# The end of attention in an adaLN block: operand placement, banks, order and softmax scaling of the last batch's outputs

## The chip, the cores and the metric

The kernel runs on one core of one Trainium2 chip. A core has five engines with instruction queues of their own: TensorE (PE: matmuls; its weight loads, PEld, overlap them), VectorE (DVE), ScalarE (ACT), GpSimd (POOL) and SyncE (SP, which here issues most DMAs). They run beside each other and wait for one another through semaphores. The metric is the device time of one execution in microseconds.

## The reference

All in float32. B = 8 batches of S = 1024 tokens, width D = 256, 16 heads of 64, 8 experts.

```python
mod = (silu(c) @ wmod).reshape(8, 6, 1, 256)      # sa, ca, ga, sb, cb, gb per batch
h = layernorm(x) * (1 + ca) + sa
q, k, v = heads(h @ w_qkv)                         # 16 heads of 64
o = softmax(q @ k.T / 8) @ v
x = x + ga * (concat(o) @ w_o)
h = layernorm(x) * (1 + cb) + sb                   # 8192 tokens
scores = softmax(h @ router_w + router_b)          # 8192 x 8
G, idx = top_k(scores.T, 512)                      # 512 tokens for each expert
y = scatter_add over idx of G * (relu(h[idx] @ w1 + b1) @ w2 + b2)
out = x + gb * y
```

The choice of 512 of 8192 tokens for each expert needs the scores of all eight batches: no expert can start before the last token's score.

## The kernel before

**Attention.** Work is cut into 128 units (`NSU`): a unit is one batch b, one pair of heads p (8 pairs, `NP`) and one half h of the 1024 queries. Inside a unit eight chunks of 128 keys pass through scores (PE, L372), a copy to SBUF (ACT, L381), a running maximum (DVE, L386), subtraction of the row maximum (DVE, L434), exp (ACT, L437), the product with the values (PE, L446) and the sum of the exponentials (POOL, L465). The loop counts g, four steps to a unit. The order of the instructions on each engine is the order in which the program writes them down; side work is hung into it by hand with `at(g, slot, function, ...)`, where the slots of one step are load, m1, post, pool and m2, in this order.

**Softmax denominators.** A unit's sums are added over the partitions by PE (`den_out`, L481), copied (L489) and stored to DRAM (`den_store`, L498). For each pair they come back spread over 128 partitions (`den_load`, L505), DVE inverts them and they are stored again (`den_inv`, L512), and come back once more broadcast to all rows (`den_spread`, L521, the tile `rb`). POOL multiplies the pair's output `oT` by them (`den_mul`, L527), and `oT` goes to DRAM (`oT_d`, L531). For the last pair of the last batch the same trip is made for each half by itself: `last_load_den` (L538), `last_inv` (L544 to L551, the tile `rb_last`) and `last_mul` (DVE, L557). Half 0 goes over SP's queue, half 1 over ACT's. Pairs 6 and 7 of the last batch stay on the chip (`at_hand`).

**Outputs of a batch.** For batches 0 to 6, attention of batch b + 1 carries them along, a tile of 128 tokens at a time: `out_load` reads x and the eight pairs (`ot`), `out_proj` multiplies by `wo` (PE, L582), then come the gate, the residual and the statistics, `out_norm` (rstd and three passes on POOL), `out_turn` (two tiles transposed, ACT copies), `out_route` (router logits, PE L637, and DVE L642 to L644), `out_exp` (ACT, L652), `out_score` (DVE: sum L659, reciprocal L660, and L663, which writes exp times reciprocal into the last 8 columns of the token's `row`), and `out_store` (POOL copies these columns into the table `scores`, L670; SP stores the row, L671).

**The last batch** has no attention after it. At the loop's end `last_gates` scales `wo` by the batch's gate (DVE, L690), `last_load` (L697) reads pairs 0 to 5 of each token tile, 384 KB for each of eight tiles, at steps 4*NSU+3 and 4*NSU+4, and L827 reads x in two halves. Then PE adds up the tiles: pairs 0 to 6 of tiles 0 to 3, then pair 7 of these, which needs `last_mul(0)`, then tiles 4 to 7 with all pairs (`add_pairs`, L854). The eight sums lie in `pos`, in banks of four pools of PSUM. `add_x` (DVE L862, statistics L116 and L117, rstd on POOL, L106 and L108), `norm` (L871 on DVE, L875 and L876 on POOL for even tiles and on DVE for odd ones), `turn`, `route` and `score` follow in an order written out by hand (L897 to L904).

**After it.** Four transposes (L983) turn the table into `p_sc`, DVE takes the upper halves of the score bits (`half`, L995), and a search finds the 512th largest score of each expert; then the tokens are gathered and the FFN of the eight experts runs. `rows_d` holds the tokens' rows in DRAM for this.

Of the kernel before, what the change touches and what calls it, by code (L numbers as in the profile page):

```python
# [28 lines left out]
F32 = mybir.dt.float32  # L29
# [10 lines left out]
P = 128  # L40
# [4 lines left out]
def adaln_block(  # L45
# [90 lines left out]
    H0 = 4  # L136
    wqs = [wp.tile([P, KC, 3, n, N], F32, name=f"wq{i}") for i, n in enumerate((H0, H - H0))]
    wo = wp.tile([P, NP, D], F32, name="wo")
# [300 lines left out]
    def values_mm(u, c):  # L439
        b, p, h = unit(u)  # L440
        if c == 0:
            avs[u] = ps_av.tile([P, QB], F32, tag="av", name=f"av{u}")
        v, pT = vs[b, p // 2], probs[u, c]
        for j in range(2):
            hh = 2 * (p % 2) + j
            nc.tensor.matmul(  # L446
                avs[u][j * N : (j + 1) * N, :], v[:, c, hh * N : (hh + 1) * N], pT[:, j, :],
                start=(c == 0), stop=(c == NT - 1),
            )

    def values_out(u):
        b, p, h = unit(u)
        if h == 0:
            oTs[b, p] = work.tile([P, S], F32, tag="oT", name=f"oT{b}_{p}", bufs=2)
        nc.scalar.copy(oTs[b, p][:, h * QB : (h + 1) * QB], avs.pop(u))  # L455
# [11 lines left out]
    den_d, rden_d = {}, {}  # L467
    at_hand = {(B - 1, p): None for p in (NP - 2, NP - 1)}

# [16 lines left out]
    def den_store(u, pd):  # L486
# [6 lines left out]
        else:  # L493
            if h == 0:
                den_d[b, p] = dram.tile([2, S], F32, name=f"den_d{b}_{p}")
            dst = den_d[b, p][:, h * QB : (h + 1) * QB]
        eng = nc.scalar if u == NSU - 1 else nc.sync
        eng.dma_start(dst.rearrange("j (i q) -> j i q", i=2), den[::32, :])  # L498
# [55 lines left out]

    def last_mul(h):
        half = oTs[B - 1, NP - 1][:, h * QB : (h + 1) * QB]
        nc.vector.tensor_mul(half, half, last_d[h])  # L557
# [97 lines left out]
    def out_score(b, t):  # L655
        n = f"{b}_{t}"
        ex = o_x.pop((b, t))
        den = small.tile([P, 2], F32, tag="rden2", name=f"rd{n}")
        nc.vector.tensor_reduce(den, ex, AX.X, ALU.add)  # L659
        nc.vector.reciprocal(den, den)  # L660
        for i in range(2):
            row = o_h[b, t + i]
            nc.vector.tensor_scalar_mul(row[:, D:], ex[:, i, :], den[:, i : i + 1])  # L663

    def out_store(b, t):
        tt = b * NT + t
        for i in range(2):
            row = o_h.pop((b, t + i))
            ct, ci = divmod(tt + i, KT)
            nc.gpsimd.tensor_copy(scores[:, ci, :, ct], row[:, D:])  # L670
            nc.sync.dma_start(rows_d[(tt + i) * P : (tt + i + 1) * P, :ROW], row)  # L671
# [21 lines left out]

    def last_load(t):
        b = B - 1
        o_t[b, t] = work.tile([P, NP - 2, P], F32, tag="p", name=f"ot{b}_{t}", bufs=PB)
        nc.sync.dma_start(  # L697
            o_t[b, t], oT_d[b][: NP - 2, :, t * P : (t + 1) * P].rearrange("n p s -> p n s")
        )

# [60 lines left out]
    at(4 * NSU - 2, "load", last_mods)  # L761
    for t in range(NT):
        at(4 * NSU + (3 if t < NT // 2 else 4), "load", last_load, t)
    at(4 * NSU + 4, "load", last_load_den, 0)
# [3 lines left out]
    with tc.manual_schedule():  # L768
# [14 lines left out]
        while g < 4 * NSU + LAG or steps:  # L783
# [12 lines left out]
            if gm == 3 and late:  # L796
                subtract(*late[1])
            run(g, "m1")
            run(g, "post")
# [4 lines left out]

            alone = turn and g not in taken
            if 0 <= u1 < NSU:
                for c in (2 * gm1, 2 * gm1 + 1):
                    if alone and c % 2:
                        max_turn(u)
                    values_mm(u1, c)  # L810
# [13 lines left out]
        b = B - 1  # L824
        for i in range(2):
            xs = work.tile([P, 4, D], F32, tag="p", name=f"xs{i}", bufs=PB)
            nc.sync.dma_start(  # L827
                xs, x[b, i * 4 * P : (i + 1) * 4 * P, :].rearrange("(t p) d -> p t d", p=P)
            )
            for t in range(4):  # L830
                o_x[b, 4 * i + t] = xs[:, t : t + 1, :]
        pd_last = ps_m.tile([P, QH], F32, tag="mm", name="pd_last")
# [6 lines left out]

        pos = []  # L840
        for pool, tag, n in (
            (ps_s, "s", 2), (ps_s, "s", 2), (ps_b, "less", 2), (ps_m, "mm", 1), (ps_av, "av", 1)
        ):
            po = pool.tile([P, n, 512], F32, tag=tag, name=f"po_last{len(pos)}")
            pos += [po[:, i, :D] for i in range(n)]

        def add_pairs(t, p0, p1):
            for p in range(p0, p1):
                src = (
                    o_t[b, t][:, p, :] if p < NP - 2  # L850
                    else (at_hand[b, p] if p == NP - 2 else oTs[b, p])[:, t * P : (t + 1) * P]
                )
                for m in range(2):
# [5 lines left out]
        def add_x(t):  # L859

            x1 = o_x[b, t]
            nc.vector.tensor_add(x1[:, 0, :], x1[:, 0, :], pos[t])  # L862
            nc.sync.dma_start(out[b, t * P : (t + 1) * P, :], x1[:, 0, :])
            mv = stats_of(small, x1, 1, f"b{b}_{t}")
            o_h[b, t] = mv, rstd_of(small, mv, 1, f"b{b}_{t}")

        def norm(t):
            mv, rs = o_h[b, t]
            row = small.tile([P, ROW], F32, tag="row", name=f"row{b}_{t}", bufs=6)
            h2 = row[:, :D]  # L870
            nc.vector.tensor_scalar(  # L871
                h2, o_x.pop((b, t))[:, 0, :], mv[:, 0, 0:1], rs, op0=ALU.subtract, op1=ALU.mult
            )
            eng = nc.vector if t % 2 else nc.gpsimd
            eng.tensor_tensor(h2, h2, mods[b][:, 2, :], ALU.mult)  # L875
            eng.tensor_tensor(h2, h2, mods[b][:, 1, :], ALU.add)  # L876
            o_h[b, t] = row

        def turn(t):
            out_turn(ps_s, b, t, tag="s")  # L880

        def route(t):
            out_route(ps_s, b, t, tag="s")

# [4 lines left out]

        half = NT // 2  # L890
        for t in range(half):
            add_pairs(t, 0, NP - 1)
        last_mul(0)
        for t in range(half):
            add_pairs(t, NP - 1, NP)
        last_mul(1)
        for f, *args in (  # L897
            (add_x, 0), (add_x, 1), (norm, 0), (add_pairs, 4, 0, NP), (add_x, 2), (norm, 1),
            (add_x, 3), (norm, 2), (add_pairs, 5, 0, NP), (turn, 0), (norm, 3), (add_x, 4),
            (route, 0), (norm, 4), (add_pairs, 6, 0, NP), (turn, 2), (add_x, 5), (norm, 5),  # L900
            (score, 0), (route, 2), (add_pairs, 7, 0, NP), (turn, 4), (add_x, 6), (norm, 6),
            (score, 2), (add_x, 7), (route, 4), (norm, 7), (score, 4), (turn, 6), (route, 6),
            (score, 6),
        ):  # L904
            f(*args)
# [33 lines left out]
    with tc.tile_pool(name="search", bufs=2) as se, tc.tile_pool(  # L939
# [49 lines left out]
        with tc.manual_schedule():  # L989
# [4 lines left out]
            low = po_.tile([P, K], U16, name="low")  # L994
            nc.vector.tensor_single_scalar(half[:, 0, :], bits, LB, op=ALU.logical_shift_right)  # L995
            nc.vector.tensor_copy(top, half[:, 0, :])
# [268 lines left out]
```

## Time and profile before

| | us |
|---|---|
| median of 3 runs (lowest, highest) | 3542.25 (3541.15, 3543.44) |
| the profiled execution, and its span | 3543.85, 3542.1 |
| busy in the span: PE, DVE, POOL, ACT | 3446.4, 2847.9, 2655.7, 2437.0 |
| loop of attention ends on PE, tile 7's last matmul ends, `half` ends | about 3182, 3221, 3233.6 |

The span is what the profiler recorded from the first to the last instruction; the profiled execution took 1.75 us more. The page's second part cuts the span into 40 slices of 88.6 us; a digit is the busy share of a slice in tenths, and PEclk the clock that TensorE was granted:

```profile
PE   8999999999999999999999999999999999995898
DVE  6888888888888888888888888888888888886332
PEclk9999999999999999999999999999999999996899
```

Slices 1 to 35 are attention, slice 36 holds the last batch's outputs and the beginning of the search, and the rest is the search, the gathering and the FFN. A line of the timeline gives the start, the length, the engine (SPq and ACTq: a DMA issued from that queue), the line of the code, the operation with its tiles, the number of instructions joined in it, and in brackets the idle time of the engine before it and what ended that.

### The profile page before, as it was taken

How to read it: one execution, taken by the hardware profiler on the slowest of the kernel's cores; microseconds unless marked ns; L12 is line 12 of the kernel's file. 1: busy time of each engine (PE TensorE's matmuls, PEld its weight loads, DVE VectorE, ACT ScalarE, POOL GpSimd, SP SyncE). 2: the span in 40 equal slices, each digit the busy share in tenths (PEclk: the TensorE clock that was granted, in tenths of full speed). 3: DMA queues.
4: the chain of work that ended last, by engine and by line, in shares of the span. 5: the costliest groups of instructions: out<-in, count | busy, mean ns of one | idle time of the engine just before them, and what ended most of it. 6: DMA issues, size and time to landing. Idle time of an engine off the chain costs nothing. (4 is left out here: it accounts for less than half of the span.)

```text
span 3542.1 us, 54875 instructions
## 1 busy us (share of the span) xinstructions
PE 3446.4 (97%) x20991; PEld 1456.2 (41%) x20991; DVE 2847.9 (80%) x3566; ACT 2437.0 (69%) x2998; POOL 2655.7 (75%) x1535
## 2 busy tenths in 40 slices
PE   8999999999999999999999999999999999995898
PEld 3333333334433343334433343334433343434566
DVE  6888888888888888888888888888888888886332
ACT  5877877777777777777777777777777777760111
POOL 3788777978788887978788888978788888881233
PEclk9999999999999999999999999999999999996899
DMA  4010012011210112011210112011210112124342
GB/s 79 14 42 31 25 46 65 26 44 44 64 54 27 52 50 65 30 41 44 64 52 28 51 50 65 31 40 47 62 51 31 48 52 58 40 78 161 95 104 43
DMA packets 190139, 185.44 MB, mean 52 GB/s; under 512 B 49308, under 2 KB 167596, under 8 KB 189748
## 3 DMA queue, kind: packets, MB, share of 16 engines
q1 hardware_dynamic: 173916, 160.54, 16.5%
q0 software_dynamic: 7168, 12.72, 1.8%
q10 hardware_dynamic: 8792, 8.67, 0.8%
q8 instruction: 165, 2.70, 0.3%
q14 instruction: 98, 0.80, 0.1%
HBM read 127.06 MB, written 63.21 MB: 54 GB/s over the span
## 5 line engine op out<-in xcount | busy, mean ns | idle before, releaser
L465 POOL TENSOR_TENSOR acc<-acc,p 128x1024 f32<-128x1024 f32 x764 | 1811.6, 2371 | 351.0 <-ACT p L437 317.6
L381 ACT COPY p<-s 128x1024 f32<-128x1024 f32 x1024 | 994.4, 1018 | 402.6 <-PE s L372 395.3
L434 DVE TENSOR_TENSOR p<-p,less 128x1024 f32<-128x1024 f32 x1024 | 1205.9, 1209 | 28.3 <-PE less L431 25.7
L386 DVE TENSOR_TENSOR top<-top,s 128x1024 f32<-128x1024 f32 x768 | 936.4, 1219 | 268.8 <-ACT p L381 228.8
L437 ACT ACTIVATE p<-p 128x1024 f32<-128x1024 f32 x1024 | 1041.8, 1057 | 72.8 <-DVE p L434 72.6
L372 PE MATMUL s<-qk,qk 64*128 64x512 f32 x4096 | 1020.3, 611 | 15.3 <-DVE parts L412 12.2
L446 PE MATMUL av<-p,v 128*64 128x512 f32 x4096 | 969.1, 593 | 1.8 <-ACT oT L455 1.8
L372 PEld LDWEIGHTS s<-qk,qk 64*128 64x128 f32 x4096 | 359.2, 186 | 512.7 <-issue 220.9
L337 PE MATMUL pq<-hT,wq 128*64 128x512 f32 x2048 | 497.0, 606 | 2.2 <-ACT hT L302 2.2
L446 PEld LDWEIGHTS av<-p,v 128*64 128x64 f32 x4096 | 279.7, 137 | 456.4 <-issue 355.4
L462 POOL TENSOR_TENSOR acc<-p,p 128x1024 f32<-128x1024 f32 x128 | 304.0, 2375 | 162.7 <-ACT p L437 162.7
L337 PEld LDWEIGHTS pq<-hT,wq 128*64 128x64 f32 x2048 | 124.9, 136 | 340.7 <-issue 204.6
L354 PE MATMUL pv<-wq,hT 128*64 128x256 f32 x2048 | 249.2, 385 | 0.0
L582 PE MATMUL po<-wo,ot 128*64 128x256 f32 x1792 | 205.7, 382 | 0.0
L354 PEld LDWEIGHTS pv<-wq,hT 128*64 128x64 f32 x2048 | 135.7, 136 | 152.3 <-issue 61.2
L1185 ACT ACTIVATE h<-ph,b_sb 128x512 f32<-128x512 f32 (+1 forms) x72 | 46.0, 640 | 209.2 <-PE ph L1181 209.2
L404 DVE TENSOR_REDUCE tt<-tt 128x8 f32<-128x1024 f32 x112 | 137.7, 1229 | 56.9 <-PE tt L393 56.8
L386 DVE TENSOR_TENSOR top<-p,s 128x1024 f32<-128x1024 f32 x128 | 155.5, 1215 | 11.9 <-ACT p L381 11.9
L393 PEld LDWEIGHTS tt<-ident,top 128*128 128x128 f32 x1024 | 109.6, 140 | 109.8 <-DVE top L386 109.8
L527 POOL TENSOR_TENSOR oT<-oT,rb 128x1024 f32<-128x1024 f32 x63 | 150.2, 2384 | 0.8 <-issue 0.8
L582 PEld LDWEIGHTS po<-wo,ot 128*64 128x64 f32 x1792 | 123.5, 137 | 66.2 <-issue 9.4
L393 PE MATMUL tt<-ident,top 128*128 128x128 f32 x1024 | 139.9, 280 | 4.7 <-DVE top L386 4.6
(191 smaller groups left out, 2298.1 us busy)
## 6 DMA issues: line engine op xcount, KB each, us to landing
rb<-rden_d SPq DMA_DIRECT2D x126, 256.0 KB
oT_d<-oT SPq DMA_DIRECT2D x62, 512.0 KB
ot<-oT_d SPq DMA_DIRECT2D x56, 512.0 KB
rows_d<-row SPq DMA_DIRECT2D x64, 132.0 KB
rows_d<-gb_d SPq DMA_DIRECT2D x8, 1024.0 KB
w<-in_L_ffn_w_dram ACTq DMA_DIRECT2D x8, 1024.0 KB
w<-in_L_ffn_w_dram SPq DMA_DIRECT2D x8, 1024.0 KB
lnx<-in_L_attn_inputs_dram SPq DMA_DIRECT2D x28, 256.0 KB
```

What stands on the lines that cost most here:

```text
L337: nc.tensor.matmul(pq[m * N : (m + 1) * N, :], wq_of(k, a, 2 * p + m), hTs[b][:, k, sl], start=(k == 0), stop=(k == KC - 1),)
L354: nc.tensor.matmul(pv[m * N : (m + 1) * N, i, :], hTs[b][:, k, t0 : t0 + N], wq_of(k, 2, 4 * g, 4), start=(k == 0), stop=(k == KC - 1),)
L372: nc.tensor.matmul(ps[:, j, :], kt[r, c * P : (c + 1) * P], qt[r, h * QB : (h + 1) * QB], start=True, stop=True,)
L381: nc.scalar.copy(probs[u, c], ps)
L386: nc.vector.tensor_tensor(tops[u], probs[u, 0] if c == 1 else tops[u], ps, ALU.max)
L393: nc.tensor.transpose(turned[u][:, 4 * j + t, :], top[:, j, t * P : (t + 1) * P], ident)
L434: nc.vector.tensor_tensor(probs[u, c], probs[u, c], less[u], ALU.add)
L437: nc.scalar.activation(probs[u, c], probs[u, c], AF.Exp)
L446: nc.tensor.matmul(avs[u][j * N : (j + 1) * N, :], v[:, c, hh * N : (hh + 1) * N], pT[:, j, :], start=(c == 0), stop=(c == NT - 1),)
L462: nc.gpsimd.tensor_tensor(sums[u], pts[0], pts[1], ALU.add)
L465: nc.gpsimd.tensor_tensor(sums[u], sums[u], pt, ALU.add)
L582: nc.tensor.matmul(po[m * N : (m + 1) * N, :], ot[:, p, m * N : (m + 1) * N], wo[:, p, :], start=(p == 0), stop=(p == NP - 1),)
```

## The change

- **Scaling of the scores.** `out_score` no longer writes into the rows. A new function `to_table` multiplies both tiles' exponentials by their reciprocals in one instruction, straight into `scores`: on POOL (in `out_store`) for batches 0 to 6, on DVE (in `out_score`) for the last. POOL then copies from the table into the rows, not the other way.
- **Operands of the last batch.** Pairs 4 to 7 stay on the chip: 4 and 5 in one tile of the tag `hT`, which is free by then, so their stores to `oT_d` go. Pairs 0 to 3 come in one load of 2 MB into the place of `wq1`, and x in one load of 1 MB into a buffer of the tag `v`, both on SP at step 4*NSU-6, where eight loads of 384 KB and two of x stood at and behind 4*NSU+3.
- **Queue.** The denominators of unit 126 are stored from ACT's queue, as those of unit 127 were.
- **Banks.** The last unit's values are summed in a bank of `ps_s`. The eight tiles lie as the list in the diff says, the transposes in `ps_m` and the logits in `ps_av`. Rows of tiles 6 and 7 lie in the place of `wq0`.
- **Order.** Pairs 0 to 6 are done for three tiles ahead of pair 7, not four. `last_mul(1)` stands behind `norm(1)`. `turn(4)` stands ahead of tile 7's matmuls. The hand-written list is rewritten to match.
- **Normalization.** Two instructions of DVE for a tile, (x - mean) * (1 + cb) in `add_x` and then * rstd + sb in `norm`, take the place of three on DVE or POOL.
- **`half`** is written in two parts of 256 columns.
- In the main loop, the transposes of the maxima go between the value products only where projections stand in the same step (`between`).

```diff
     H0 = 4
-    wqs = [wp.tile([P, KC, 3, n, N], F32, name=f"wq{i}") for i, n in enumerate((H0, H - H0))]
+    wqs = [
+        wp.tile([P, KC, 3, n, N], F32, tag=f"wq{i}", name=f"wq{i}")
+        for i, n in enumerate((H0, H - H0))
+    ]
     wo = wp.tile([P, NP, D], F32, name="wo")
 ...
     def values_mm(u, c):
         b, p, h = unit(u)
         if c == 0:
-            avs[u] = ps_av.tile([P, QB], F32, tag="av", name=f"av{u}")
+            pool, tag = (ps_s, "s") if u == NSU - 1 else (ps_av, "av")
+            avs[u] = pool.tile([P, QB], F32, tag=tag, name=f"av{u}")
 ...
     def values_out(u):
         b, p, h = unit(u)
-        if h == 0:
+        if h == 0 and (b, p) == (B - 1, NP - 4):
+            two = work.tile([P, 2, S], F32, tag="hT", name=f"oT{b}_{p}")
+            oTs[b, p], oTs[b, p + 1] = two[:, 0, :], two[:, 1, :]
+        elif h == 0 and (b, p) != (B - 1, NP - 3):
             oTs[b, p] = work.tile([P, S], F32, tag="oT", name=f"oT{b}_{p}", bufs=2)
         nc.scalar.copy(oTs[b, p][:, h * QB : (h + 1) * QB], avs.pop(u))
 ...
     den_d, rden_d = {}, {}
-    at_hand = {(B - 1, p): None for p in (NP - 2, NP - 1)}
+    at_hand = {(B - 1, p): None for p in range(NP - 4, NP)}
 ...
-        eng = nc.scalar if u == NSU - 1 else nc.sync
+        eng = nc.scalar if u >= NSU - 2 else nc.sync
         eng.dma_start(dst.rearrange("j (i q) -> j i q", i=2), den[::32, :])
 ...
     def last_mul(h):
+        at_hand[B - 1, NP - 1] = oTs[B - 1, NP - 1]
         half = oTs[B - 1, NP - 1][:, h * QB : (h + 1) * QB]
         nc.vector.tensor_mul(half, half, last_d[h])
     def out_score(b, t):
         n = f"{b}_{t}"
-        ex = o_x.pop((b, t))
+        ex = o_x[b, t]
         den = small.tile([P, 2], F32, tag="rden2", name=f"rd{n}")
         nc.vector.tensor_reduce(den, ex, AX.X, ALU.add)
         nc.vector.reciprocal(den, den)
-        for i in range(2):
-            row = o_h[b, t + i]
-            nc.vector.tensor_scalar_mul(row[:, D:], ex[:, i, :], den[:, i : i + 1])
+        o_x[b, t] = ex, den
+        if b == B - 1:
+            to_table(b, t, nc.vector)
+    def to_table(b, t, eng):
+        ex, den = o_x.pop((b, t))
+        ct, ci = divmod(b * NT + t, KT)
+        eng.tensor_tensor(
+            scores[:, ci : ci + 2, :, ct], ex, den.unsqueeze(2).to_broadcast([P, 2, E]), ALU.mult
+        )
     def out_store(b, t):
+        if b < B - 1:
+            to_table(b, t, nc.gpsimd)
         tt = b * NT + t
         for i in range(2):
             row = o_h.pop((b, t + i))
             ct, ci = divmod(tt + i, KT)
-            nc.gpsimd.tensor_copy(scores[:, ci, :, ct], row[:, D:])
+            nc.gpsimd.tensor_copy(row[:, D:], scores[:, ci, :, ct])
             nc.sync.dma_start(rows_d[(tt + i) * P : (tt + i + 1) * P, :ROW], row)
 ...
-    def last_load(t):
-        b = B - 1
-        o_t[b, t] = work.tile([P, NP - 2, P], F32, tag="p", name=f"ot{b}_{t}", bufs=PB)
-        nc.sync.dma_start(
-            o_t[b, t], oT_d[b][: NP - 2, :, t * P : (t + 1) * P].rearrange("n p s -> p n s")
-        )
+    last = {}
+    def last_load():
+        b, n = B - 1, NP - 4
+        last["oT"] = wp.tile([P, n, S], F32, tag="wq1", name="oT_last")
+        nc.sync.dma_start(last["oT"], oT_d[b][:n].rearrange("n p s -> p n s"))
+        last["x"] = work.tile([P, NT, D], F32, tag="v", name="x_last")
+        nc.sync.dma_start(last["x"], x[b].rearrange("(t p) d -> p t d", p=P))
 ...
-    for t in range(NT):
-        at(4 * NSU + (3 if t < NT // 2 else 4), "load", last_load, t)
+    at(4 * NSU - 6, "load", last_load)
     at(4 * NSU + 4, "load", last_load_den, 0)
 ...
         b = B - 1
-        for i in range(2):
-            xs = work.tile([P, 4, D], F32, tag="p", name=f"xs{i}", bufs=PB)
-            nc.sync.dma_start(
-                xs, x[b, i * 4 * P : (i + 1) * 4 * P, :].rearrange("(t p) d -> p t d", p=P)
-            )
-            for t in range(4):
-                o_x[b, 4 * i + t] = xs[:, t : t + 1, :]
+        rows_last = wp.tile([P, 2, ROW], F32, tag="wq0", name="rows_last")
         pd_last = ps_m.tile([P, QH], F32, tag="mm", name="pd_last")
 ...
-        pos = []
-        for pool, tag, n in (
-            (ps_s, "s", 2), (ps_s, "s", 2), (ps_b, "less", 2), (ps_m, "mm", 1), (ps_av, "av", 1)
+        pos = {}
+        for pool, tag, ts in (
+            (ps_s, "s", (0, 1)), (ps_m, "mm", (2,)), (ps_av, "av", (3,)), (ps_s, "s", (4, 6)),
+            (ps_b, "less", (5, 7)),
         ):
-            po = pool.tile([P, n, 512], F32, tag=tag, name=f"po_last{len(pos)}")
-            pos += [po[:, i, :D] for i in range(n)]
+            po = pool.tile([P, len(ts), 512], F32, tag=tag, name=f"po_last{ts[0]}")
+            for i, t in enumerate(ts):
+                pos[t] = po[:, i, :D]
         def add_pairs(t, p0, p1):
             for p in range(p0, p1):
-                src = (
-                    o_t[b, t][:, p, :] if p < NP - 2
-                    else (at_hand[b, p] if p == NP - 2 else oTs[b, p])[:, t * P : (t + 1) * P]
-                )
+                src = last["oT"][:, p, :] if p < NP - 4 else at_hand[b, p]
+                src = src[:, t * P : (t + 1) * P]
 ...
         def add_x(t):
-            x1 = o_x[b, t]
+            x1 = last["x"][:, t : t + 1, :]
             nc.vector.tensor_add(x1[:, 0, :], x1[:, 0, :], pos[t])
             nc.sync.dma_start(out[b, t * P : (t + 1) * P, :], x1[:, 0, :])
             mv = stats_of(small, x1, 1, f"b{b}_{t}")
-            o_h[b, t] = mv, rstd_of(small, mv, 1, f"b{b}_{t}")
+            rs = rstd_of(small, mv, 1, f"b{b}_{t}")
+            if t < NT - 2:
+                row = small.tile([P, ROW], F32, tag="row", name=f"row{b}_{t}", bufs=6)
+            else:
+                row = rows_last[:, t - NT + 2, :]
+            nc.vector.scalar_tensor_tensor(
+                row[:, :D], x1[:, 0, :], mv[:, 0, 0:1], mods[b][:, 2, :],
+                op0=ALU.subtract, op1=ALU.mult,
+            )
+            o_h[b, t] = row, rs
         def norm(t):
-            mv, rs = o_h[b, t]
-            row = small.tile([P, ROW], F32, tag="row", name=f"row{b}_{t}", bufs=6)
-            h2 = row[:, :D]
-            nc.vector.tensor_scalar(
-                h2, o_x.pop((b, t))[:, 0, :], mv[:, 0, 0:1], rs, op0=ALU.subtract, op1=ALU.mult
-            )
-            eng = nc.vector if t % 2 else nc.gpsimd
-            eng.tensor_tensor(h2, h2, mods[b][:, 2, :], ALU.mult)
-            eng.tensor_tensor(h2, h2, mods[b][:, 1, :], ALU.add)
+            row, rs = o_h[b, t]
+            nc.vector.scalar_tensor_tensor(
+                row[:, :D], row[:, :D], rs, mods[b][:, 1, :], op0=ALU.mult, op1=ALU.add
+            )
             o_h[b, t] = row
         def turn(t):
-            out_turn(ps_s, b, t, tag="s")
+            out_turn(ps_m, b, t, tag="mm")
         def route(t):
-            out_route(ps_s, b, t, tag="s")
+            out_route(ps_av, b, t, tag="av")
 ...
-        half = NT // 2
-        for t in range(half):
+        n = 3
+        for t in range(n):
             add_pairs(t, 0, NP - 1)
         last_mul(0)
-        for t in range(half):
+        for t in range(n):
             add_pairs(t, NP - 1, NP)
-        last_mul(1)
         for f, *args in (
-            (add_x, 0), (add_x, 1), (norm, 0), (add_pairs, 4, 0, NP), (add_x, 2), (norm, 1),
-            (add_x, 3), (norm, 2), (add_pairs, 5, 0, NP), (turn, 0), (norm, 3), (add_x, 4),
-            (route, 0), (norm, 4), (add_pairs, 6, 0, NP), (turn, 2), (add_x, 5), (norm, 5),
-            (score, 0), (route, 2), (add_pairs, 7, 0, NP), (turn, 4), (add_x, 6), (norm, 6),
-            (score, 2), (add_x, 7), (route, 4), (norm, 7), (score, 4), (turn, 6), (route, 6),
-            (score, 6),
+            (add_x, 0), (add_pairs, 3, 0, NP), (add_x, 1), (norm, 0), (add_x, 2), (norm, 1),
+            (last_mul, 1), (norm, 2), (add_x, 3), (add_pairs, 4, 0, NP), (norm, 3), (turn, 0),
+            (add_x, 4), (norm, 4), (add_pairs, 5, 0, NP), (add_x, 5), (route, 0), (norm, 5),
+            (turn, 2), (add_pairs, 6, 0, NP), (score, 0), (add_x, 6), (route, 2), (norm, 6),
+            (turn, 4), (add_pairs, 7, 0, NP), (score, 2), (add_x, 7), (route, 4), (norm, 7),
+            (score, 4), (turn, 6), (route, 6), (score, 6),
         ):
             f(*args)
 ...
-            nc.vector.tensor_single_scalar(half[:, 0, :], bits, LB, op=ALU.logical_shift_right)
+            for s in (slice(0, K // 2), slice(K // 2, K)):
+                nc.vector.tensor_single_scalar(
+                    half[:, 0, s], bits[:, s], LB, op=ALU.logical_shift_right
+                )
 ...
```

## The prediction

> **What bounds the kernel now.** I read the page's first rows, then a table of busy time by stretches, then the timeline of the last 60 us of attention. The stretches first (columns: window, length, busy time of each engine with its instruction count, granted TensorE clock, DMA share, GB/s):
>
> ```profile
> 3000.00:3100.00 100.00, 99.55 (x606) 40.03 (x604) 83.90 (x98) 75.62 (x93) 81.73 (x45) 1.00 0.13 41
> 3150.00:3200.00 50.00, 40.52 (x310) 18.09 (x311) 34.69 (x39) 25.07 (x32) 33.34 (x16) 1.00 0.46 116
> 3200.00:3220.00 20.00, 18.59 (x178) 11.92 (x175) 14.02 (x41) 1.56 (x4) 9.51 (x20) 0.91 0.25 82
> 3220.00:3240.00 20.00, 8.63 (x128) 6.04 (x124) 12.09 (x50) 2.54 (x8) 7.63 (x32) 0.61 0.69 239
> ```
>
> Inside attention TensorE (PE, the first engine column) is busy 99.6 of 100 us, so what the change does on DVE and GpSimd (POOL) there is worth something only if PE waited for it. From 3150 on PE has gaps. The timeline tells what they wait for (start, length, engine, line, idle before and its releaser):
>
> ```profile
> 3177.78 2.48 DVE L663 TENSOR_SCALAR row<-ex,rd 128x8 f32<-128x8 f32 x2
> 3180.18 4.51 DVE L690 TENSOR_TENSOR wo<-wo,mod 128x1024 f32<-128x1024 f32 x2
> ...
> 3182.24 4.07 SPq L697 DMA_DIRECT2D ot<-oT_d  x4
> 3182.53 0.60 ACTq L498 DMA_DIRECT2D den_d<-den  x1
> ...
> 3187.45 0.38 ACTq L538 DMA_DIRECT2D dq_last<-den_d  x1
> ...
> 3192.50 0.43 DVE L544 RECIPROCAL dq_last<-dq_last 128x8 f32<-128x8 f32 x2 [7.81 <-DMA dq_last<-den_d]
> ...
> 3198.84 1.29 DVE L557 TENSOR_TENSOR oT<-oT,rb_last 128x512 f32<-128x512 f32 x2 [5.91 <-DMA rows_d<-row]
> 3199.59 2.73 PE L854 MATMUL po_last<-wo,oT 128*64 128x256 f32 x16 [4.26 <-DVE oT L557]
> ```
>
> The denominators of pair 7 make two trips through DRAM, and their 2 to 4 KB stand behind 3.1 MB of `ot` loads: 4.9 us from store to the next issue (3182.53 to 3187.45), 4.7 more to the reciprocal. PE does pairs 0–6 of four tiles meanwhile, runs dry, waits 4.26 us, and restarts slowly. After the last tile:
>
> ```profile
> 3223.35 0.41 DVE L862 TENSOR_TENSOR xs<-xs,po_last 128x256 f32<-128x256 f32 x1
> ...
> 3226.78 0.69 PE L618 MATMUL pth<-ident,row 128*128 128x128 f32 x2 [3.06 <-DVE row L876]
> ...
> 3228.21 1.03 PE L637 MATMUL pl<-rw,h2T 128*64 128x8 f32 x16
> ...
> 3231.93 0.33 POOL L670 COPY scores<-row 128x8 f32<-128x8 f32 x2
> ...
> 3232.91 0.69 DVE L995 TENSOR_SCALAR half<-p_sc 128x512 int32<-128x512 int32 x1 [1.65 <-PE p_sc L983]
> ```
>
> Tile 7's matmuls end at 3220.99 (tile timeline), and its add waits until 3223.35 behind tile 2/3's scores on DVE. A serial chain then runs to the table of score bits (`half`, done 3233.60). From there on the same search and FFN run in both kernels, so I place the end of `half` and shift the rest.
>
> **The sum, A: to the first three tiles.** PE is free of the last denominator matmul at 3182.16. The store of unit 126 moves to ACT's queue, between the den copy and the last exps: one issue, 0.60 to 0.75 (ACT row at 3182.53): PE starts at 3182.9. `wo` is ready: without the 2.48 of L663 its scaling ends near 3182.3 instead of 3184.7, so the 0.64 + 0.60 that PE waited there is gone. One tile with seven pairs is 3.02 (starts 3185.88, 3188.90, 3191.92). Three of them (four before): 3191.9; 12 matmuls of pair 7 at 0.108: 3193.2. The factor for half 0 must be multiplied in by 3191.9. Half 0's den copy ends at 3176.62 (timeline, L489), its store then leaves ACT at once, not at 3181.05 behind SP's `ot` issues. Without the loads I take the hops at the quiet figures of this trace: store to next issue 1.65 (pair 6: 3168.36 to 3170.01), load to reciprocal at most 2.4, reciprocal's store to the spread 2.4 (3173.03 to 3175.44); spread to use 4.6, though measured in the tail (3194.26 to 3198.84). Half 0: load 3178.4, reciprocal behind the `wo` scaling 3182.5, spread 3183 to 3185.3, landed 3187.6 to 3189.9. DVE still does half 1's reciprocal first: store 3183.2, load 3184.8, reciprocal 3187.2. So the multiply is done between 3188.3 and 3190.6: slack 1.3 to 3.6. Half 1's multiply, now behind tile 1's norm on DVE, ends about 3198.7; tile 4, which needs it, comes at 3199.7. What is behind it on DVE is tile 2's norm, and after that only tile 4's chain, so 1 us late costs at most 1.
>
> **B: to the end of tile 7.** Five tiles of eight pairs at 3.45 (3.02 x 8/7), three transposes at 0.66, two routers at 0.64 (L618, L637 warm): 20.5, end 3213.9. That is 7.1 before 3220.99. It consists of the 4.26 wait, 1.2 in front, and the slow restart (granted clock 0.5–0.65 there; 16 matmuls took 2.73 instead of 1.73), less what ACT's issue costs. The new order puts no more into PE in this stretch: `pth_4` moves ahead of tile 7 (as much as leaves).
>
> **C: tile 7 to `half`.** The add starts at once: scores 2/3 were exponentiated before, since `pth_4`'s copy no longer stands in ACT ahead of them. Add and statistics 1.05 (0.41+0.43+0.18), rstd on POOL with hops 0.95 (0.19+0.55). The three passes (0.41+0.43+0.43) become one before and one behind rstd, the first beside POOL: 0.45. Here no row is near: L1083, the same operation, took 0.76 at 512 elements, L862 took 0.41 at 256. I take 0.45 by the size; the ends are 0.40 and 0.75. Transpose 0.7, copy 0.65, router 0.9 (cold 1.03), logits to reciprocal 1.4 (3229.28 to 3230.60), one product into the table 0.2 in place of two multiplies and two POOL copies (1.65, 3230.63 to 3232.26). Then four transposes L983: two stood early before, now all four are last, 1.43. `half` in two passes 0.85. Sum 8.6, before 12.6. Gain 4.0, so `half` is done at 3222.5, 11.1 before 3233.60.
>
> The split of `half`: both halves read what the last transpose writes, so nothing overlaps. The row: L862, 256 elements from PSUM, 0.412; twice is 0.82 against 0.69, +0.13. The Trainium skill ("VectorE: DVE Perf Modes", section on the TRN2 errata) says each instruction pays a fixed cost and gives (N+151)/0.96 ns for an f32 add: 0.424 twice, 0.85, +0.16. It speaks against this edit; 0.02 between them. I take the skill's, as it also gives L995's 0.69.
>
> **Steady state: nothing.** L663 leaves DVE in 28 pairs (about 1.8 each inside attention); POOL gets a product of 128x16 instead (between 0.2 and 0.45, from L670 and L106). PE waits for neither: it was 99.6% busy. POOL idles 1.25 after such a store (before L106 at 1151.74). If that cover were gone, 28 x 0.25 to 0.45 = 7 to 13.
>
> **The early loads.** 3 MB enter SP's queue at about 3128.5, behind `dq` of pair 5, and past them go `rden` (3135.09) and `rb` of pair 5 (3136.50 until about 3141); POOL uses `rb` at 3148.79. At the 290 GB/s that the `ot` loads made, they are done by 3141: `rb` lands by 3147. Cost zero; the upper end is below. Eight `ot` and two `xs` loads go, and two stores of 512 KB.
>
> The den store on ACT's queue: the skill ("DMA: Bandwidth & Descriptors", section "Issuing engines are not separate DMA queues") says that queues of all issuers share the same 16 DMA engines, so another issuer saves only issue time. By it the edit gains nothing and costs its 0.7 on ACT; by a queue of its own it would have saved some 4. The row decides: half 1's chain ran wholly on ACT before, and was as slow (3182.53 to 3187.45, and to about 3192.7) as half 0's on SP. I count -0.7, and the hop's gain to the loads' going.
>
> **Total.** 3543.85 (profiled run; span 3542.1 and 1.75 around it) less 11.1 is 3532.8; the median lies 1.6 below that run: 3542.25 - 11.1 = **3531.2**.
>
> **Rivals.**
> *Half the gain.* If half 1's 4.9 and 5.2 are fixed latency, not load, its reciprocal comes at 3193.3, half 0's multiply right behind it, and PE waits until about 3194.2 (-2.3); and if the new DVE form takes 0.75, DVE with 2 x 0.75 + 1.05 + scores a tile comes near PE's 3.45 (-2.4 over the stretch). Gain 6.4: 3535.9. For it: the releaser of the 7.81 is a DMA. Against: pair 6's quick hops. 0.12.
> *Slower: the early loads hold up `rb` of pair 5.* If 3 MB take much longer than at 290 GB/s, POOL stands at L527, its sums come late, and the last den matmul with them: 1.2 us of slack there (POOL's last sum ends 3180.24, used 3181.4). All 11 us are eaten once `rb` lands at 3161, that is below about 120 GB/s; at 90 GB/s the loads last until 3163, `rb` lands about 3169, 8 after break-even: 3542 + 8 = 3550. For it: `x` and `oT` come in rows of 1 to 4 KB per partition, on one queue with the small ones. Against: 290 to 298 GB/s elsewhere. 0.05.
> *The scaling counts in the steady state after all.* If PE's 12.2 us on L412 shrinks with DVE's load: 28 x 0.2, 5.6 more, 3525.6. 0.04. That the edit has no effect there is my forecast.
>
> **Numbers.** Forecast 0.79, rivals as given. Differences under 0.2% (7.1 us) I count as no change, as a measurement of this kernel can tell no less. The forecast's own bounds: hops +1, DVE form 0 to +2.5, ACT's issue 0 to +0.7, clock +1, and -3 if the tail overlaps better: 3528 to 3535. With half the gain inside: 3527 to 3537.5. Faster 0.86 (forecast, steady-state gain, and a quarter of the half-gain case), same 0.09, slower 0.05.
>
> **What would show it.** A: no PE wait over 1 us between 3183 and 3214; half 1's reciprocal near 3187. B: tile 7 ends near 3214. C: 8.6 from there to `half`. L527 for pair 5 at 3148.8 or less, else the loads did harm. PE idle in 1000–3100 as before, within 3 us. I am wrong if PE waits at pair 7 of tile 0, or if L527 is late.

## The result, and the profile after

The changed kernel took 3532.35 us (median of 8 runs, 3530.72 to 3533.85) beside 3542.6 of the kernel before (8 runs, 3539.87 to 3543.59): a ratio of 0.9972 with a 95% interval of 0.9963 to 0.9981. The medians lie 10.25 us apart. The profiled span fell from 3542.1 to 3530.5. The forecast was 3531.2, with bounds of 3528 and 3535.

The slices of the page show next to nothing. PE's slice 36 (counted from 0) goes from 5 to 6 tenths, and its granted clock there from 6 to 7:

```profile
PE   8999999999999999999999999999999999996898
PEclk9999999999999999999999999999999999997899
```

The timeline of the changed kernel's tail shows where the time went. The lines answer to those of the prediction; the matmuls of `add_pairs` are now L871, the add is L879, the reciprocal L552, `half` L1016:

```profile
3177.18 0.60 ACTq L506 DMA_DIRECT2D den_d<-den  x1
...
3179.42 0.33 SPq L546 DMA_DIRECT2D dq_last<-den_d  x1
...
3183.20 1.95 PE L871 MATMUL po_last<-wo,oT_last 128*64 128x256 f32 x16
...
3188.14 0.20 DVE L552 RECIPROCAL dq_last<-dq_last 128x8 f32<-128x8 f32 x1 [5.26 <-DMA dq_last<-den_d]
3188.27 0.69 DVE L566 TENSOR_TENSOR oT<-oT,rb_last 128x512 f32<-128x512 f32 x1
...
3191.02 2.76 PE L871 MATMUL po_last<-wo,oT 128*64 128x256 f32 x24
...
3212.19 1.90 PE L871 MATMUL po_last<-wo,oT 128*64 128x256 f32 x16
...
3214.14 0.42 DVE L879 TENSOR_TENSOR x_last<-x_last,po_last 128x256 f32<-128x256 f32 x1 [1.29 <-PE po_last L871]
...
3215.27 0.48 DVE L887 SCALAR_TENSOR_TENSOR rows_last<-x_last,mv_b,mod 128x256 f32<-128x256 f32 x1
3215.33 0.48 POOL L106 TENSOR_SCALAR ve_b<-mv_b 128x1 f32<-128x1 f32 x1 [2.09 <-DVE mv_b L117]
...
3219.09 0.44 PE L1003 MATMUL p_sc<-ident,scores 128*128 128x128 f32 x2 [0.28 <-DVE lg L651]
...
3220.26 0.32 DVE L677 TENSOR_TENSOR scores<-ex,rd 128x16 f32<-128x16 f32 x1
...
3220.73 0.66 PE L1003 MATMUL p_sc<-ident,scores 128*128 128x128 f32 x2 [1.20 <-POOL mine L991]
...
3221.43 0.75 DVE L1016 TENSOR_SCALAR half<-p_sc 128x256 int32<-128x256 int32 x2 [0.85 <-PE p_sc L1003]
```

The reciprocal at 3188.14 is half 1's; half 0's came at 3182.69. Half 0's multiply (L566) ends at 3188.96, and PE needs it at about 3192.3: the 24 matmuls at 3191.02 run on from pair 6 of tile 2 into pair 7 without a gap. The 4.26 us wait of before is gone, and so is the slow restart. Tile 7's matmuls end at 3214.09 (before 3220.99), its add starts 0.05 later (before 2.36), and `half` is done at 3222.18 (before 3233.60).

**A yardstick.** The profiled executions differ by up to 1.2 us on their way to the tail (x7 below, whose edit acts earlier, aside). I therefore count from the start of GpSimd's last but one sum of exponentials (L465, later L473; 3175.39 before, 3175.99 after) to the end of `half`: 58.21 us before, 46.19 after, 12.02 less. Behind `half` the same code took 307.2 to 308.5 us in all thirteen profiled executions. So a span can't tell a difference under 1 us. Two profiles of the changed kernel agree within 0.01 us on the yardstick; of the kernel before there is one profile, and the 12.02 rests on it.

### The profile page after: what moved, and what is told of

Its sections match the earlier page's. It is cut to its first block, busy times and chain, and to the rows that moved or that the text cites. A ratio compares the mean times of both kernels' runs of the same rounds, so it can differ in the third digit from the quotient of the medians.

```text
span 3530.5 us, 54857 instructions
## 1 busy us (share of the span) xinstructions
PE 3444.8 (98%) x20991; PEld 1454.9 (41%) x20991; DVE 2796.1 (79%) x3507; ACT 2438.1 (69%) x2998; POOL 2664.6 (75%) x1555
## 5 line engine op out<-in xcount | busy, mean ns | idle before, releaser
L473 POOL TENSOR_TENSOR acc<-acc,p 128x1024 f32<-128x1024 f32 x764 | 1811.7, 2371 | 351.9 <-ACT p L440 318.6
```

Source lines behind the costliest of these rows:

```text
L473: nc.gpsimd.tensor_tensor(sums[u], sums[u], pt, ALU.add)
```

## Experiments

Each is one edit to the changed kernel. All medians were measured beside the kernel before.

| run | what is different | median | span | yardstick, against 46.19 |
|---|---|---|---|---|
| x11 | nothing | 3531.69 | 3529.9 | 46.18, -0.01 |
| x1 | 3.1 MB of traffic at the old place | 3540.19 | 3538.4 | 53.70, +7.51 |
| x9 | the same bytes in 4 KB rows | 3536.01 | 3534.3 | 50.34, +4.15 |
| x10 | the same pieces, 8 B each | 3531.81 | 3530.2 | 46.17, -0.02 |
| x7 | 4 MB more behind the early loads | 3539.24 | 3537.9 | its start is itself late |
| x2 | unit 126's store on SP | 3531.38 | 3529.3 | 45.51, -0.68 |
| x3 | scaling of batches 0 to 6 as before | 3532.38 | 3530.6 | 46.63, +0.44 |
| x5 | `turn(4)` behind tile 7 | 3533.65 | 3532.1 | 48.42, +2.23 |
| x4 | last scores over GpSimd | 3532.73 | 3530.3 | 47.19, +1.00 |
| x6 | three passes of normalization | 3532.79 | 3529.5 | 46.93, +0.74 |
| x8b | three repairs | 3531.52 | 3529.1 | 45.07, -1.12 |

The repeat:

> The changed kernel once more, to know how far one profiled execution differs from the next and as the base of the next run: span 3530.0 to 3531.0, tile 7's last matmul to the end of half 8.0 to 8.2 us, median within 1 us of 3532.35.

Chain (8.10) and median came as expected, and the span of 3529.9 is 0.1 under the range.

### The bytes of the late loads (x1, x9, x10)

x1 puts the old loads back as traffic that nobody reads:

```diff
+    def dummy_load(t):
+        tile = work.tile([P, NP - 2, P], F32, tag="p", name=f"dm{t}", bufs=PB)
+        nc.sync.dma_start(
+            tile, oT_d[B - 2][: NP - 2, :, t * P : (t + 1) * P].rearrange("n p s -> p n s")
+        )
...
+    for t in range(NT):
+        at(4 * NSU + (3 if t < NT // 2 else 4), "load", dummy_load, t)
```

> The changed kernel with the eight loads of 384 KB of the kernel before put back at their old steps, as pure traffic (the previous batch's pairs into buffers nobody reads). Load theory (mine): the trips of the denominators stand behind these bytes; the reciprocal of half 1 comes at 3192 to 3193.5 in place of 3188.1, PE waits 1.5 to 3 us ahead of pair 7 of tile 0 and restarts slowly; tile 7 ends at 3216 to 3219 (3214.1 without), span 3532.5 to 3535.5. Fixed-latency theory (half-the-gain rival): the hops don't care; reciprocal at 3188 to 3189, no wait of PE, span 3530 to 3531.

The load theory held in kind, and was too small in size. The timeline of x1:

```profile
3176.83 9.35 SPq L726 DMA_DIRECT2D dm<-oT_d  x8
...
3184.24 0.49 ACTq L506 DMA_DIRECT2D den_d<-den  x1
...
3186.23 1.27 SPq L546 DMA_DIRECT2D dq_last<-den_d  x1
...
3188.83 0.38 ACTq L546 DMA_DIRECT2D dq_last<-den_d  x1
...
3191.41 0.20 DVE L552 RECIPROCAL dq_last<-dq_last 128x8 f32<-128x8 f32 x1 [8.10 <-DMA dq_last<-den_d]
...
3197.09 0.69 DVE L566 TENSOR_TENSOR oT<-oT,rb_last 128x512 f32<-128x512 f32 x1 [4.40 <-DMA rb_last<-rden_last]
3197.84 2.83 PE L879 MATMUL po_last<-wo,oT 128*64 128x256 f32 x12 [4.85 <-DVE oT L566]
```

The lines show which trip decides. Half 1's reciprocal, on ACT's queue, came at 3192.49 as expected: its hop from store to load grew from 1.70 us (3183.73 to 3185.43 in the changed kernel) to 4.59, though the traffic is on SP's queue. But half 0's load leaves SP at 3186.23 in place of 3179.42, and its factor arrives at 3197, so PE waits 4.85 us and not 1.5 to 3, and its 12 matmuls then take 2.83. The 16 behind them take 3.10 in place of 1.90. The traffic alone costs 7.51 us. Up to tile 7's last matmul the change had won 7.50 (45.60 and 38.10 after the yardstick's start). That the two agree is chance: in x1 the wait cost 4.85 and the slow matmuls behind it about 2.5 (28 took 5.55 us from the first to the next, at 0.108 each 3.02), in the kernel before 4.26 and about 1.7 (40 took 6.05, at 0.108 each 4.32).

Is it the bytes, or that SP is busy issuing for 9.35 us? x9 moves the same bytes in six loads (`oT_d[B - 2][t]` into `[P, S]` tiles, 4 KB rows), x10 issues x1's pieces with 8 B in each (`tile[:, :, :2]`).

> The same 3.1 MB of pure traffic at the same steps as in x1, but in six loads of 512 KB whose rows are 4 KB (x1: eight loads with pieces of 512 B). Issue theory: in x1 SP needed 9.35 us to issue and half 0's load stood behind it; here SP is free by 3180, half 0's reciprocal comes by 3184, PE does not wait, span within 0.7 of the changed kernel's 3530.5. Byte theory: the bytes themselves hold the trips up, whatever issues them: half 0's reciprocal at 3186 to 3188, its multiply at 3192.5 to 3194.5, PE waits 0.5 to 2.5 us, span 3531 to 3534.

> The eight loads of x1 at the same steps with all their pieces, but 8 B in each in place of 512 B: SP has as many pieces to issue, the DMA engines next to no bytes. Issue theory: SP again needs about 9 us, half 0's load leaves at about 3186, its reciprocal comes at 3188 to 3189, its multiply at 3193 to 3195, PE waits 1 to 3 us; span 3532 to 3535. Byte theory: with the bytes gone the trips are as quick as in the changed kernel; half 0's reciprocal by 3184, no wait, span within 0.7 of 3530.5.

The timeline of x9, and then of x10:

```profile
3181.28 0.67 SPq L546 DMA_DIRECT2D dq_last<-den_d  x1
...
3189.01 0.20 DVE L552 RECIPROCAL dq_last<-dq_last 128x8 f32<-128x8 f32 x1 [6.02 <-DMA dq_last<-den_d]
...
3194.90 2.17 PE L877 MATMUL po_last<-wo,oT 128*64 128x256 f32 x12 [2.22 <-DVE oT L566]
```

```profile
3176.28 5.94 SPq L726 DMA_DIRECT2D dm<-oT_d  x8
...
3182.27 0.55 SPq L546 DMA_DIRECT2D dq_last<-den_d  x1
...
3184.13 0.20 DVE L552 RECIPROCAL dq_last<-dq_last 128x8 f32<-128x8 f32 x1 [1.35 <-DMA dq_last<-den_d]
```

With bytes and an early issue (x9) the 4 KB take 7.7 us from issue to reciprocal (3181.28 to 3189.01), and PE waits 2.22; with a late issue and no bytes (x10) they take 1.9, and PE doesn't wait. So the bytes hold the trips up, and issuing the pieces alone does no harm. Without bytes SP also issues the same pieces in 5.94 us in place of 9.35, so in x1 the bytes act twice: half 0's load leaves late, and its trip is slow. x9's reciprocal came 1 us later than I had expected, and its span is 0.3 over my range. It costs 4.15 and not 7.51: half 0's load leaves SP 4.95 us earlier than in x1, and the rows move faster than x1's pieces (398 GB/s in 3182 to 3186, beside 293). Which of the two counts for more wasn't tested.

### The early loads as a danger (x7)

```diff
         nc.sync.dma_start(last["x"], x[b].rearrange("(t p) d -> p t d", p=P))
+        spare_d = dram.tile([NP, P, S], F32, name="spare_d")
+        nc.sync.dma_start(spare_d, oT_d[B - 2])
```

> The changed kernel with 4 MB more (a copy from DRAM to DRAM that nobody reads) issued right behind the early loads, ahead of pair 5's trip. Queue theory (my rival of the slower side, its mechanism): the two small transfers of pair 5 wait until the bytes ahead are through; the hop from rden to rb grows from 4.8 to over 12 us, GpSimd's multiply of pair 5 comes at 3155 to 3170 in place of 3149.4, and the end moves with it: span 3535 to 3548. Interleaving theory: small transfers pass between the large ones, hop under 8, multiply by 3152, span within 1 us of 3530.5.

The windows of the changed kernel at its early loads (the last number is GB/s), and then its timeline for pair 5:

```profile
3129.00:3132.00 3.00, 2.74 (x14) 0.70 (x12) 2.90 (x4) 3.00 (x4) 3.00 (x2) 1.00 0.95 304
3132.00:3135.00 3.00, 2.60 (x12) 0.69 (x12) 2.90 (x3) 2.97 (x4) 2.41 (x2) 1.00 1.00 399
3135.00:3138.00 3.00, 2.80 (x14) 0.79 (x12) 2.90 (x5) 2.22 (x3) 2.92 (x2) 1.00 1.03 371
```

```profile
3135.70 0.33 SPq L520 DMA_DIRECT2D rden_d<-dq  x1
...
3140.47 1.15 SPq L529 DMA_DIRECT2D rb<-rden_d  x2
...
3149.39 2.37 POOL L535 TENSOR_TENSOR oT<-oT,rb 128x1024 f32<-128x1024 f32 x1
```

The same in x7:

```profile
3136.21 0.34 SPq L520 DMA_DIRECT2D rden_d<-dq  x1
...
3152.31 1.14 SPq L529 DMA_DIRECT2D rb<-rden_d  x2
...
3157.00 2.37 POOL L535 TENSOR_TENSOR oT<-oT,rb 128x1024 f32<-128x1024 f32 x1 [7.05 <-DMA rb<-rden_d]
```

Pair 5's hop from `rden` to `rb` was 1.41 us before (3135.09 to 3136.50), is 4.77 with the early loads, and 16.10 with 4 MB more. The queue theory holds: in x7 the core moves 350 GB/s in 3141 to 3150 and 8 in 3150 to 3153, and the spread is issued at 3152.31. GpSimd waits 7.05 us, and the span grows by 7.4, so next to nothing behind the multiply takes any of it up: of the 1.2 us of slack that the prediction put there, 0.2 show at most (x7's yardstick is 45.97). The mechanism of the slower rival is real; the change stays clear of it. From the spread's issue to the multiply x7 needed 4.7 us; by this estimate the spread lands at about 3145 in the changed kernel, 4 us ahead of its use.

The multiply's start is 0.60 later than before (3149.39 and 3148.79), which the prediction named as a sign of harm. But this profile was already 0.69 later at 3100 (a sum of exponentials starts at 3099.31 before and at 3100.00 after), and GpSimd didn't wait ahead of the multiply. The early loads did no harm.

### The store on ACT's queue (x2)

```diff
-        eng = nc.scalar if u >= NSU - 2 else nc.sync
+        eng = nc.scalar if u == NSU - 1 else nc.sync
```

> The changed kernel with the denominator store of unit 126 back on SP's queue. Mine: SP is free now, so the store leaves at 3177.2 as on ACT; ACT's last two exps start 0.5 to 0.7 earlier and PE's first output matmul too (3182.5 to 3182.7 in place of 3183.2); span 3529.8 to 3530.1, a difference that only the trace can show. Rival (the queue matters): half 0's trip takes over 1 us longer, its reciprocal comes after 3184, and nothing is won.

ACT's exponentials behind the copy in the changed kernel, and then in x2:

```profile
3177.83 2.00 ACT L440 ACTIVATE p<-p 128x1024 f32<-128x1024 f32 x2 [0.68 <-ACT den L497]
```

```profile
3176.59 2.10 ACT L440 ACTIVATE p<-p 128x1024 f32<-128x1024 f32 x2
```

The store left SP at 3176.72, 0.03 after the copy, half 0's reciprocal came at 3182.24, and PE started at 3182.05. Against the yardstick's start this is 0.69 earlier, and `half` is 0.68 earlier. This profile reached the yardstick 0.46 earlier than the changed kernel's, which explains most of PE's start and the span (3529.3) lying under my ranges. With the loads gone SP had the time, so the edit of the queue costs what it puts on ACT and brings nothing.

### The scaling in the steady state (x3)

```diff
+        else:
+            o_x.pop((b, t))
+            for i in range(2):
+                row = o_h[b, t + i]
+                nc.vector.tensor_scalar_mul(row[:, D:], ex[:, i, :], den[:, i : i + 1])
```

(and in `out_store` the copies from the rows into the table, for these batches.)

> The changed kernel with the scaling of batches 0 to 6 as before (DVE writes two products into the rows, GpSimd copies them into the table); the last batch stays as changed. Mine: PE's busy time up to 3100 is the same within 1 us; only the last pair's two products (2 to 2.5 us) stand ahead of the wo scaling again, PE waits 0.5 to 1.3 us in the first output tile; span 3531 to 3532. Rival (the scaling counts in the steady state): PE loses 3 to 6 us along the loop, span 3534 to 3536.

One window of the changed kernel, and then of x3 (PE, PEld, DVE, ACT, POOL):

```profile
2000.00:2500.00 500.00, 498.03 (x3034) 200.92 (x3032) 416.20 (x502) 372.79 (x458) 406.74 (x237) 1.00 0.17 49
```

```profile
2000.00:2500.00 500.00, 497.99 (x3034) 200.90 (x3032) 426.89 (x514) 372.61 (x458) 404.13 (x231) 1.00 0.16 48
```

In x3 DVE has 10.7 us more to do in 500, GpSimd 2.6 less, and PE's busy time differs by 0.04. Over 0 to 3100 PE was busy 3074.52 before, 3074.90 after and 3074.69 in x3. The edit does nothing in the steady state. At the end it brings 0.44, somewhat less than I expected: the 2.48 us of products stand ahead of the `wo` scaling again, but PE waits only 0.21 for it and runs its next matmuls about 0.4 later, since it starts with pairs 0 to 3, whose half of `wo` is scaled first:

```profile
3185.52 1.52 PE L877 MATMUL po_last<-wo,oT 128*64 128x256 f32 x12 [0.21 <-DVE wo L714]
```

### The chain from tile 7 to `half` (x5, x4, x6)

x5 exchanges two steps of the list:

```diff
-            (turn, 4), (add_pairs, 7, 0, NP), (score, 2), (add_x, 7), (route, 4), (norm, 7),
+            (add_pairs, 7, 0, NP), (turn, 4), (score, 2), (add_x, 7), (route, 4), (norm, 7),
```

> The changed kernel with tile 4 and 5's transposes behind tile 7's matmuls again, as in the kernel before. Mine: the exponentials of tiles 2 and 3 wait in ACT behind the copy of these transposes, DVE's scores behind the exponentials and tile 7's add behind the scores: its add starts 2 to 2.6 us after tile 7's last matmul in place of 0.05, and the chain from there to the end of half grows from 8.1 to between 10 and 10.8. Rival: the add is held only by the engines' own work and starts within 1 us; the chain stays under 9.2.

The timeline of x5:

```profile
3212.80 0.66 PE L627 MATMUL pth<-ident,row 128*128 128x128 f32 x4
3213.55 0.59 ACT L636 COPY h2T<-pth 128x512 f32<-128x512 f32 x1 [6.41 <-PE pth L627]
3214.03 0.49 ACT L661 ACTIVATE ex<-lg,rnm 128x8 f32<-128x8 f32 x2
...
3214.96 0.18 DVE L677 TENSOR_TENSOR scores<-ex,rd 128x16 f32<-128x16 f32 x1
...
3215.05 0.41 DVE L879 TENSOR_TENSOR x_last<-x_last,po_last 128x256 f32<-128x256 f32 x1
```

Here the order on three engines can be read downwards: transposes, copy, exponentials, scores, and only then tile 7's add, 2.18 us after the last matmul (3212.87). The chain is 11.0, a little over the range, and tile 7 ends 0.7 earlier without the transposes ahead of it, so 2.23 remain.

x4 writes the last batch's scores into the rows on DVE and lets GpSimd copy them into the table (x3's edit, with `b == B - 1`). x6 makes three passes behind the reciprocal standard deviation, as the lines that the change removes in `norm`.

> The changed kernel with the last batch's scores as before: DVE writes two products into the rows, GpSimd copies them into the table. Mine: the chain from tile 7's last matmul to the end of half grows from 8.1 to 9.3 to 9.7 us (two products 0.36 and two copies with hops 0.65 to 1.3 in place of one product). Rival: GpSimd is also building the search's constants there, its copies queue behind them, and the chain grows to over 10.5.

> The changed kernel with three passes behind the reciprocal deviation (on DVE for odd tiles, on GpSimd for even ones the last two), as before. Mine: the chain from tile 7 to half grows from 8.1 by 0.6 to 0.9 us; the start of tile 7 does not move by more than 0.3. Rival (DVE or GpSimd set the pace of the tiles): PE waits between tiles 4 and 7 and tile 7's last matmul comes over 1 us later too.

x4's chain was 9.10 us, 1.0 more than 8.09 and just under my range; x6's was 8.85, 0.76 more, and tile 7 ended at the same point of the yardstick (38.08 and 38.10 after its start), so the passes don't set the pace of the tiles. Both rivals fell.

### Three repairs (x8b)

x2's edit, `half` in one pass, and epsilon added on DVE:

```diff
-            rs = rstd_of(small, mv, 1, f"b{b}_{t}")
+            ve = small.tile([P, 1], F32, tag="ve", name=f"ve_b{b}_{t}")
+            nc.vector.tensor_scalar(ve, mv[:, :, 1], EPS, 1.0, op0=ALU.add, op1=ALU.mult)
+            rs = small.tile([P, 1], F32, tag="rs", name=f"rs_b{b}_{t}")
+            nc.gpsimd.tensor_tensor(rs, ve, mhalf[:, :1], ALU.pow)
```

> The changed kernel with three repairs that the runs point to: the denominator store of unit 126 back on SP, half taken in one pass, and the variance's epsilon added on DVE, so that GpSimd has one instruction of the reciprocal deviation and not two. Mine: PE's first output matmul 0.6 to 0.7 earlier against the loop's end, tile 7 to half 7.6 to 7.9 in place of 8.1, span 3529.0 to 3530.0; too little to be seen in the medians (under 0.05%). Rival: the extra DVE instruction delays the rows of the tiles and PE waits between tiles; tile 7 ends later than in x2.

PE starts 0.72 earlier against the yardstick's start, the chain is 7.68 us, `half` comes 1.12 earlier: about as expected. In the medians it can't be told from the changed kernel (3531.52 beside 3531.69 of x11). By its one trace it is the best of the kernels.

## Why the prediction was right

The forecast lies 1.15 us under the measured median, inside its bounds, and its mechanism held: with the large loads gone from the tail, PE didn't wait for pair 7, and the serial chain behind tile 7 became shorter. In absolute times A and B agree within 0.3 us, partly by luck, since the profile after reached the yardstick's start 0.60 later than the one before.

- **A, to the first three tiles.** PE started at 3183.20 (3182.9 foretold), half 0's multiply was done at 3188.96 (3188.3 to 3190.6), and PE didn't wait. The cause was tested: x1 gives 7.51 us back, and x9 and x10 show that it is the bytes. What was mis-sized is the price of a failure: the rival counted 2.3 us for slow hops of half 1, and x1 shows that under load half 0's trip is the later one, with a wait of 4.85. Too large was the term for `wo`: 0.64 + 0.60 foretold, and x3 gives back 0.44. The 0.60 of the trace before is idle time ahead of the first weight load (3182.13), which waited for nothing that the profile shows, and so not for `wo`. Half 1's reciprocal came 0.9 late (3188.14, not 3187.2): its store left 0.5 later, and from the load's issue it took 2.71, about as pair 6's did (3170.01 to 3172.76); the 2.4 left out the time of the issue itself. It cost nothing: half 1's multiply ended at 3199.47, and tile 4's pair 7 follows at about 3200.1.
- **The store on ACT** was counted at -0.7 against the new order's gain; x2 measures 0.68. That the Trainium skill ("DMA: Bandwidth & Descriptors", section "Issuing engines are not separate DMA queues") sees no more than issue time in another queue fits x2, where going back to SP loses nothing.
- **B, to the end of tile 7.** 3213.9 foretold, 3214.09 measured. The terms add up to 3213.7 (3193.2 + 20.5); that slip hides a part of the 0.60 by which this profile is later. From tile 3's start to tile 7's end PE took 20.48 us, as foretold. The list of what the gain consists of was incomplete. In the kernel before, PE also waited twice for ACT's copy of the transposes ahead of a router, 1.41 us in all; now a tile's matmuls stand between `turn` and `route`, and the router doesn't wait. Two lines of before, and one of after:

```profile
3211.39 0.64 PE L637 MATMUL pl<-rw,h2T 128*64 128x8 f32 x16 [0.68 <-ACT h2T L627]
...
3216.85 0.64 PE L637 MATMUL pl<-rw,h2T 128*64 128x8 f32 x16 [0.73 <-ACT h2T L627]
```

```profile
3204.70 0.59 PE L646 MATMUL pl<-rw,h2T 128*64 128x8 f32 x16
```

- **C, tile 7 to `half`.** 8.6 foretold, 8.09 measured, with terms off both ways. Two of the four transposes L983 (now L1003) are done at 3219.09, while PE waits for the last scores: I had all four in the chain, 0.7 too much. The router's matmuls took 0.64 at a granted clock of 1.00 (3218 to 3219), where I had taken 0.9. Against that, from the statistics to the last pass it took 1.24 (3215.23 to 3216.47) and not 0.95, and the last product into the table 0.32 and not 0.2. In x6, where DVE makes no pass over the row beside it, the 0.95 came out (3214.60 to 3215.55). The new form took 0.48 (0.45 foretold, 0.75 in the rival). `half` in two passes took 0.75, and not 0.85.
- **The split of `half`.** Each part takes 0.42, as L862 did. The formula of the Trainium skill ("VectorE: DVE Perf Modes", section on the TRN2 errata) gives 0.424 as an estimate, though the page states it for an add and its fixed cost for sources in SBUF, and these parts read PSUM. But the second part starts 0.09 before the first ends. So two cost 0.06 more than one (0.69), and not 0.13 or 0.16. The edit does cost, and very little.
- **Steady state** nothing, as foretold (x3). **The early loads** cost nothing, at 304 to 399 GB/s in place of the 290 I had taken, and with their danger where I had put it (x7).

The parts taken back one by one make 7.51 + 2.23 + 1.00 + 0.74 + 0.44 - 0.68 = 11.24 of 12.02 us. The sum is no full account: x1's 7.51 is more than the 6.0 us that the wait and the slow matmuls cost before. So about 2 us have no experiment of their own. In this rest lie the router's two waits (1.41, read from the trace only), a start of PE that even in x2 comes 0.25 earlier than before (6.52 and 6.77 after the yardstick's start), three tiles ahead of pair 7 in place of four, the banks, `between`, and what the parts do to each other.

## What to carry to other kernels

In these runs short dependent transfers through DRAM needed quiet DMA engines more than a queue of their own: look for a place for the large loads where a trip has slack, and work out by how much they lengthen what is queued there. A load that is early enough for its reader can be too early for its neighbours; the price is the neighbour's hop (here it grew from 1.4 to 4.8 us, with about 8 us to spare between landing and use before), and once the slack is gone it turns into time (x7: 7.05 us of wait, 7.4 of span). In the last tile of a pipeline, look on each in-order engine for what stands ahead of the serial chain: exchanging two steps was worth 2.2 us. Other work between a transpose and what needs its copy covers the copy (0.7 us a time in the trace before).

## What I had not expected of the hardware

- GpSimd's first instruction of the reciprocal standard deviation (L106, 128x1) took 0.19 us (median) before and in x6, and 0.47 to 0.48 in all eight tiles of the changed kernel, where DVE starts its first pass (L887, 0.48) just before it, and GpSimd's ends 0.06 after DVE's (3215.81 and 3215.75). The Trainium skill ("SBUF — State Buffer", section "SBUF: two separate sides") says that a DVE instruction with two inputs in SBUF and a GpSimd instruction that reads SBUF hold a shared port exclusively: the one that starts first has it for the whole instruction, and the other waits. The times fit it, and this was the rule to weigh against "the first beside POOL". x8b gives GpSimd one instruction fewer there, and the chain is 0.41 shorter: 0.22 up to the last pass (1.02 in place of 1.24), 0.06 in `half`, and most of the rest in the last product (0.19 in place of 0.32).
- The two products of 128x8 on DVE (L663) took 2.48 us inside attention beside GpSimd's sums, and 0.36 in the tail.
